# Attention with image prompts on one Trainium2 core: inner products sent through DRAM, and four smaller moves

## The chip, the core and the metric

The kernel runs on one of the eight cores of a Trainium2 chip. A core has four engines that compute, each with its own in-order instruction stream: TensorE (in the profile PE for products and PEld for loading their stationary operand), VectorE (DVE), ScalarE (ACT) and GpSimd (POOL). SyncE (SP) issues transfers. Transfers run on 16 DMA engines of the core; they are issued from the streams of SP, ACT or POOL. The metric is the device time of one execution in microseconds, the median of several runs. The profile shows one execution, taken by the hardware profiler.

## The reference

For each of 8 batch entries b there are 112 rows of x with 320 channels (20 heads of 16) and 375 rows of context with 512 features, the last four of which are image prompts. Everything is float32.

```
text, ip = ehs[:, :-4], ehs[:, -4:]                 # 371 and 4 rows
q = heads(x @ W_q);  k, v = heads(text @ W_k), heads(text @ W_v)
probs = softmax(q k^T / 4)                           # 112 x 371 for each head
text_out = probs v
attn_scores = q heads(ip @ W_k_ip)^T / 4             # 112 x 4
qsem = l2norm(probs text)                            # 112 x 512 for each head
sem  = qsem l2norm(ip)^T                             # 112 x 4
probs_ip = softmax(attn_scores + 0.5 sem) * mask
out = (text_out + probs_ip heads(ip @ W_v_ip)) @ W_out + b_out + x
```

The kernel never forms `probs text`. The squared norm of that row is p G p^T, where G is the 371 x 371 matrix of inner products of the text rows, and its product with the four normalised prompts needs only the inner products of text and prompts. So one product of p with a wide matrix [G, text times prompts, a column of ones, the head's values] gives the norm, `sem`, the sum of the exponentials and `text_out` together.

## The kernel before

The work is cut into 40 steps (b, g): 8 batch entries times 5 groups of 4 heads. The four heads of a group stand in the four quadrants of 32 partitions, so that their products run side by side.

For each b, `gram(b)` forms the upper triangle of G together with the prompts' columns on TensorE; `doubled` takes it out of PSUM with a factor of 2, and POOL multiplies the diagonal blocks by `half`. The result is `ug`, 128 partitions by 792 floats (`GW`; 3,168 bytes in a partition). The products want each 32-row block of `ug` in all four quadrants, so `gram_to_groups(b, blocks)` (L551) copies it into `u`: four transfers for each of the four blocks, 32 rows of 3,168 bytes each, from SBUF to SBUF. `values` makes the values, which go to DRAM (`vd`) and back by `values_to_groups` (L712) into `vr`, already split by quadrant; `placed` (L759, POOL) copies one group's 16 value columns behind the blocks in `u`.

For each step, `scores` (TensorE) and `probabilities` (DVE maximum, ACT exponential) give p. L821 on SP's queue places p's rows in a ring of two buffers, `xg`, one transfer a head, 28 partitions for each head. `transposed` (L823, DVE) turns `xg` by 32 x 32 blocks into `xgT`, in one piece, halves or other pieces of the 12 blocks. `multiplied` and `product` (L843) then run the 12 blocks of each head against `u`. `reduced` (DVE, L907) and `value_sums` (ACT, L881) take the sums out; `finish` ends a batch entry.

All streams are ordered by hand. The steps run in pairs: `pair(n)` works on steps n and n+1, issues the scores for n+2 and n+3, and calls `moved(b, g)` after the products of each step; `behind(n)` places the larger pieces (`k`, `v`, `gr`, `q`: keys, values, inner products, queries of coming entries) behind an even step. `moved` (L1373) issues the transfers for the next entry: for an even b block 0 after group 1, block 1 after group 2 and block 3 with the values after group 3; block 2 stands at the start of `behind`. For an odd b blocks 0 and 1 stand after groups 0 and 1, block 2 at the start of `behind` of group 1 and block 3 at its end after group 3. For entry 0 the blocks are sent in the prologue.

The prologue (L1206 to L1253) is ordered by hand too. `awake(n)` (L485) issues n products of a constant tile `waker` that nobody reads. `normalised_prompts` (L275) forms the norms of the 32 prompt rows (8 x 4) and turns the prompts twice, raw into `ipT` and normalised times 0.5 into `ipnT`; `prompt_projections` (L308) multiplies `ipT` by W_k_ip and W_v_ip much later, in `behind(0)`. The prologue calls `values_to_groups(0)` (L1235) on SP before the first group's scores and probabilities, whose rows go out on the same queue.

The waits that the prediction speaks of are at L854 (TensorE for `xgT` or `u`), at L763 (POOL for `u` or `vr`) and at L833 (DVE for `xg`).

Of the kernel before, what the change touches and what calls it, by code (L numbers as in the profile page):

```python
# [20 lines left out]
def kernel(  # L21
# [187 lines left out]

    halves(0)  # L210

    waker = const.tile([P, P], F32, tag="waker", name="waker")
    nc.vector.memset(waker, 1.0)

    hmask = const.tile([P, HC], F32, tag="hmask", name="hmask")
    nc.vector.tensor_reduce(
# [32 lines left out]
        for at in attn_ring:  # L249
            nc.gpsimd.memset(at[:, C:], 0.0)  # L250

    ipT = const.tile([P, NE, N], F32, tag="ipT", name="ipT")
    ipnT = const.tile([P, NE, N], F32, tag="ipnT", name="ipnT")
    kip = const.tile([P, NC, N], F32, tag="kip", name="kip")

# [19 lines left out]
    def normalised_prompts():  # L275

        sq = early[:, 1]
        ss = small.tile([N, 1], F32, tag="ipss", name="ipss", bufs=1)
        nc.vector.tensor_tensor_reduce(
            out=sq, in0=ip_sb, in1=ip_sb, scale=1.0, scalar=0.0, op0=ALU.mult, op1=ALU.add,  # L280
            accum_out=ss,
        )
        nc.vector.tensor_scalar_max(ss, ss, EPS * EPS)
        rn = small.tile([N, 1], F32, tag="iprn", name="iprn", bufs=1)
        yield

        ipn = early[:, 1]

        def turned_prompts(src, dst, n):
            ps = bank(f"ps_ipT{n}", spare=True)  # L290
            for e in range(NE):
                nc.tensor.transpose(
                    ps[:, e * N : (e + 1) * N], chunk(src, e), ident[:N, :N]
                )
            nc.vector.tensor_copy(
                dst, ps[:, : NE * N].rearrange("p (e n) -> p e n", n=N)
            )

        nc.scalar.activation(rn, ss, AF.Sqrt)
        turned_prompts(ip_sb, ipT, "r")  # L300
        nc.vector.reciprocal(rn, rn)
        nc.vector.tensor_scalar(ipn, ip_sb, rn, 0.5, op0=ALU.mult, op1=ALU.mult)
        yield

        turned_prompts(ipn, ipnT, "n")
        yield

    def prompt_projections():  # L308

        ps = bank("ps_kv")  # L310
        for e in range(NE):
            for i, w in enumerate((wkip_sb, wvip_sb)):
                for n, part in enumerate(parts):
                    m = 2 * i + n
                    nc.tensor.matmul(
                        ps[m * N : (m + 1) * N, : C // 2],
                        ipT[:, e, :],
                        w[:, e, part],
                        start=(e == 0),
                        stop=(e == NE - 1),  # L320
                    )
        kv = work.tile([P, CP], F32, tag="vip", name="kv", bufs=1)
        nc.scalar.copy(kv[:N, parts[0]], ps[:N, : C // 2])
        nc.scalar.copy(kv[:N, parts[1]], ps[N : 2 * N, : C // 2])
        nc.scalar.copy(kv[2 * N :, : C // 2], ps[2 * N :, : C // 2])
        nc.gpsimd.tensor_copy(kv[:N, C:], kv[:N, FULL * P : C])
        yield

        ps = bank("ps_kipT")
        for i in range(NC):  # L330
            nc.tensor.transpose(
                ps[:, i * N : (i + 1) * N], kv[:N, i * P : (i + 1) * P], ident[:N, :N]
            )
        nc.scalar.copy(kip, ps[:, : NC * N].rearrange("p (i n) -> p i n", n=N))
        for i in range(NC):
            nc.gpsimd.tensor_tensor(
                kipb[:, i],
                kip[:, i, :NIP].unsqueeze(1).to_broadcast([P, HC, NIP]),
                hmask.unsqueeze(2).to_broadcast([P, HC, NIP]),
                ALU.mult,  # L340
            )
        yield

        for n, part in enumerate(parts):
            m = 2 + n
            nc.sync.dma_start(vipd[:, part], kv[m * N : (m + 1) * N, : C // 2])
        yield
# [182 lines left out]
    def gram(b):  # L530
# [3 lines left out]
        for c in range(NT):  # L534
# [13 lines left out]
            doubled(ps, c, c, DEAL[c] if left_out(b, c) else ())  # L548
            yield

    def gram_to_groups(b, blocks, eng=nc.sync):  # L551

        for q in blocks:
            for a in range(GROUP):
                eng.dma_start(
                    st[b]["u"][a * RG : (a + 1) * RG, q * GW : (q + 1) * GW],
                    ug[q * RG : (q + 1) * RG, :],
                )
# [264 lines left out]
    def transposed(b, g, j0=0, j1=BLK):  # L823

        xg = x_ring[(b * NG + g) % NX]
        if j1 < j0 + 1:
            return
        if ("xT", g) not in st[b]:
            st[b]["xT", g] = work.tile([P, BLK, P], F32, tag="xgT", name=f"xgT_{b}_{g}")
        xT = st[b]["xT", g]  # L830
        n = BLK // (2 if b == B - 1 or (b, g) == (0, 0) or j1 - j0 < BLK else 1)
        for j in range(j0, j1, n):
            nc.vector.transpose(  # L833
                xT[:, j : j + n].rearrange("p j (k q) -> p q j k", q=QN),
                xg[:, :, j * RG : (j + n) * RG].rearrange("p q (j k) -> p q j k", k=RG),
            )
# [371 lines left out]
    products = first_gram()  # L1208
    next(prompts)
    nc.scalar.preload_act_table(AF.Sqrt)  # L1210
    awake(5)
    next(context)
    next(prompts)
    nc.scalar.preload_act_table(AF.Exp)
    load_query_weights(nc.gpsimd, range(1))
    next(context)
# [15 lines left out]
    run(("q", 0), lambda: project_queries(pairs[0]))  # L1232
    run(("k", 0), lambda: keys(0))
    run(("q", 0), None)
    values_to_groups(0)  # L1235
    for a in range(GROUP):
        scores(0, 0, a, early=True)
        probabilities(0, 0, a)
    run(("q", 0), None)
    run(("k", 0), None)  # L1240
    for a in range(GROUP):
# [63 lines left out]
    inputs = {5: (0, 2), 9: (2, 5), 19: (5, B)}  # L1305

    late = (1, 5)

    def pair(n):

        one, two = steps[n], steps[n + 1]
        b, g = one
        tags = ("mm", "sc") if b % 2 and g == NG - 1 else ("sc", "mm")
        ends = (BLK - 2, BLK - 1)

        products_in(b, g, ("qd",) * GROUP)
        for j in range(BLK - 2):
            product(b, g, j, range(GROUP))
            if j < 2:
                heads = (HIGH, LOW)[j]  # L1320
                coming_scores(n + LEAD, heads, tags[j])
                coming_probabilities(n + LEAD, heads)
            if j == 1:
                if n in late:
                    transposed(*two, 0, BLK // 2)
                transposed(*two, BLK // 2, BLK)
            if j % QN == QN - 1:
                placed(*two, (j // QN,))
        if n == 3:
            load_channels(nc.gpsimd, wo_sb, w_out)  # L1330
            nc.gpsimd.dma_start(sm_sb, smask.unsqueeze(1))
            nc.gpsimd.dma_start(bias_sb, b_out.partition_broadcast(S))
        if n in inputs:
            load_inputs(*inputs[n])
        products_in(*two, (tags[1],) * 2 + (tags[0],) * 2)
        for there, here in ((HIGH, LOW), (LOW, HIGH)):
            product(*two, 0, there)
            for j in ends:
                product(b, g, j, here)
        del st[b]["xT", g]  # L1340
        placed(*two, (NT - 1,))
        moved(b, g)
        if g > 1 and g != 2:
            turned(b + 2)
        if b % 2 and g in (0, NG - 1):
            f(b - 1 - (g == 0))
        if g in (1, 2):
            f(b - 1, 2)
        reduced(b, g)
        if g == 2:  # L1350
            turned(b + 2)
        value_sums(b, g)
        if b % 2 == 0 and b > 0 and g == 1:
            turned_inputs(pairs[b // 2 + 1], 0, FULL)

        b, g = two
        for j in range(1, BLK - 2):
            product(b, g, j, range(GROUP))
            if j == 4:
                coming_scores(n + 1 + LEAD, HIGH, "qd")  # L1360
                coming_probabilities(n + 1 + LEAD, HIGH)
            if j == 7:
                coming_scores(n + 1 + LEAD, LOW, "qd")
                coming_probabilities(n + 1 + LEAD, LOW)
        for heads in (HIGH, LOW):
            for j in ends:
                product(b, g, j, heads)
        del st[b]["xT", g]
        moved(b, g)
        if one in ((b, 2), (b, 3)):  # L1370
            turned(b + 2, 1 + (one == (0, 3)))

    def moved(b, g):  # L1373

        nb = b + 1
        if b % 2 == 0:
            if g in (1, 2):
                gram_to_groups(nb, (g - 1,))
            if g == 3:
                todo = [lambda: gram_to_groups(nb, (3,)), lambda: values_to_groups(nb)]  # L1380
                for move in reversed(todo) if nb == B - 1 else todo:
                    move()
        else:
            if g in (0, 1):
                gram_to_groups(nb, (g,))
            if g == 2:
                values_to_groups(nb, 0, 2)

    def behind(n):
# [4 lines left out]

        def tr(i):
            if i < len(two):
                transposed(*two[i], 0, BLK // (1 + i))

        if b % 2 == 0 and g == 0:
            if n == 0:  # L1400
# [257 lines left out]
```

## Time and profile before

| | us |
|---|---|
| median of 3 runs | 405.58 |
| lowest and highest run | 403.81 and 406.58 |
| profiled execution, its own time | 403.29 |
| its span, first to last instruction | 401.6 |
| ACT busy | 200.2 |
| POOL busy | 192.5 |
| `u<-ug` on SP's queue | 120 transfers |

The profiled execution was a little faster than the runs shown. Rows of a timeline begin with the start and the duration in microseconds, then the engine, the line, the operation, what is written from what, and the shapes; brackets tell the idle time before and what ended it. The letter q behind an engine's name (SPq) means that the row is the issue of a transfer, not its work. A row of the transfers gives how many were issued and the size of each. A row of the windows gives for a stretch its length, the busy time of each engine, TensorE's granted clock, the share of the 16 DMA engines that was busy and the rate in GB/s.

### The profile page before, as it was taken

To read this page: it belongs to the slowest core of one execution; us is meant where nothing else is said; L and a number is where in the kernel's file an instruction comes from. 1 tells how busy PE (TensorE), PEld (TensorE's weight loads), DVE (VectorE), ACT (ScalarE), POOL (GpSimd) and SP (SyncE) were. 2 spreads that over 40 slices of the span, in tenths; PEclk is the share of its full clock that TensorE was granted. 3 is DMA by queue.
4 is the path that set the end of the run, shared out by engine and by line. 5 is a ranking of instruction groups with operands and counts; after the bars stand their busy time and mean duration, and the time that the engine had idled before them with its cause. 6 is when DMAs were issued, how large, how long until landed. Compare 5 with 4: busy or idle time off the path is not lost.

```text
span 401.6 us, 14442 instructions
## 1 busy us (share of the span) xinstructions
PE 396.1 (99%) x5685; PEld 320.2 (80%) x5685; DVE 332.2 (83%) x712; ACT 200.2 (50%) x716; POOL 192.5 (48%) x409
## 2 busy tenths in 40 slices
PE   8999999999999999999999999999999999999996
PEld 8768697888878788878787878877887878887894
DVE  4357689877989988987999898897798988888995
ACT  3255343347434853425652665334843485446864
POOL 8655427052562567051573348432256155804781
PEclk9999999999999999999999999999999999999999
DMA  8979657988577846668657766576846544775321
GB/s 239 217 202 258 155 153 178 210 193 190 149 186 155 202 122 187 155 146 184 169 148 167 193 155 169 160 185 140 191 120 175 130 125 116 197 176 166 108 59 29
DMA packets 58119, 65.86 MB, mean 164 GB/s; under 512 B 20165, under 2 KB 51257, under 8 KB 58052
## 3 DMA queue, kind: packets, MB, share of 16 engines
q1 hardware_dynamic: 54814, 58.23, 57.7%
q0 software_dynamic: 2544, 5.92, 6.0%
q8 instruction: 45, 0.74, 0.9%
q10 hardware_dynamic: 694, 0.80, 0.6%
q14 instruction: 22, 0.18, 0.2%
HBM read 20.22 MB, written 5.22 MB: 63 GB/s over the span
## 4 chain that ended last, share of the span: by engine, by line
PE 96%; DVE 2%; ACT 1%; issue 0%; DVEq 0%
PE ps_qd L854 47%; PE ps_k L571 10%; PE ps_g L541 8%; PE ps_s L797 6%; PE ps_v L613 6%; PE ps_vs L671 6%; PE ps_k L588 3%; PE ps_q L402 3%; PE ps_o L1050 2%; PE ps_g L503 1%; DVE xgT L833 1%; PE ps_w L489 1%; PE ps_c L472 1%; PE ps_q L384 1%; PE ps_a L1041 0%
## 5 line engine op out<-in xcount | busy, mean ns | idle before, releaser
L854 PE MATMUL ps_qd<-u,xgT 32*112 32x72 f32 (+10 forms) x3806 | 216.0, 352 | 0.8 <-DVE xgT L833 0.7
L854 PEld LDWEIGHTS ps_qd<-u,xgT 32*112 32x112 f32 x3806 | 177.5, 172 | 33.5 <-issue 4.2
L833 DVE STREAM_TRANSPOSE xgT<-xg 128x768 f32<-128x768 f32 (+1 forms) x63 | 123.1, 1973 | 4.3 <-DMA xg<-p 4.1
L814 ACT ACTIVATE p<-ps_s,nmx 112x371 f32<-112x371 f32 x160 | 85.5, 585 | 64.9 <-DVE nmx L810 63.9
L810 DVE TENSOR_REDUCE nmx<-ps_s 112x1 f32<-112x371 f32 x160 | 76.8, 534 | 26.2 <-PE ps_s L797 24.6
L763 POOL COPY u<-vr 128x64 f32<-128x64 f32 x120 | 26.9, 237 | 140.8 <-PE ps_qd L854 76.8
L907 DVE CUSTOM_DVE_ANT_0 p<-ps_qd,p 112x371 f32<-112x371 f32 x148 | 71.6, 540 | 10.0 <-ACT pvs L881 7.4
L797 PE MATMUL ps_s<-kT,qm 32*112 32x375 f32 (+1 forms) x320 | 61.0, 485 | 0.0
L881 ACT COPY pvs<-ps_qd 112x21 f32<-112x21 f32 x148 | 21.3, 200 | 52.5 <-DVE ss L907 49.9
L571 PE MATMUL ps_k<-ctxT,wk_sb 128*128 128x371 f32 x128 | 43.4, 482 | 0.0
L571 PEld LDWEIGHTS ps_k<-ctxT,wk_sb 128*128 128x128 f32 x128 | 23.1, 190 | 12.8 <-issue 0.8
L541 PE MATMUL ps_g<-ctxT 128*32 128x119 f32 (+11 forms) x672 | 32.7, 338 | 0.0
L541 PEld LDWEIGHTS ps_g<-ctxT 128*32 128x32 f32 x672 | 27.7, 109 | 6.1 <-issue 1.2
L797 PEld LDWEIGHTS ps_s<-kT,qm 32*112 32x112 f32 x320 | 27.3, 171 | 6.3 <-POOL vext L675 1.1
L460 DVE STREAM_TRANSPOSE ctxT<-ct 128x512 f32<-128x512 f32 x21 | 22.5, 1081 | 6.7 <-DMA ct<-in_ctx_dram 6.7
L816 ACT COPY ipl<-ps_s 112x4 f32<-112x4 f32 x140 | 24.3, 174 | 0.0
L613 PE MATMUL ps_v<-wv_sb,ctxT 128*128 128x320 f32 x80 | 23.6, 442 | 0.0
L613 PEld LDWEIGHTS ps_v<-wv_sb,ctxT 128*128 128x128 f32 x80 | 14.5, 190 | 5.6
L578 ACT COPY kT<-ps_k 128x371 f32<-128x371 f32 x16 | 7.5, 469 | 22.2 <-PE ps_k L571 22.2
L1029 POOL TENSOR_TENSOR vip<-vip,w 112x1280 f32<-112x1280 f32 (+1 forms) x8 | 17.5, 2182 | 0.2 <-DVE w L1023 0.2
L525 POOL TENSOR_TENSOR ug<-ug,half 128x128 f32<-128x128 f32 (+1 forms) x24 | 10.7, 451 | 14.3 <-ACT ug L524 13.0
L520 ACT ACTIVATE ug<-ps_g 128x279 f32<-128x279 f32 (+5 forms) x24 | 8.0, 333 | 17.5 <-PE ps_g L541 10.8
(189 smaller groups left out, 469.1 us busy)
## 6 DMA issues: line engine op xcount, KB each, us to landing
xg<-p SPq DMA_DIRECT2D x159, 162.3 KB
u<-ug SPq DMA_DIRECT2D x120, 99.0 KB
ct<-in_ctx_dram SPq DMA_DIRECT2D x28, 176.0 KB
vip<-vipd SPq DMA_DIRECT2D x7, 560.0 KB
vr<-vd SPq DMA_DIRECT2D x20, 120.0 KB
out_dram<-ob SPq DMA_DIRECT2D x7, 140.0 KB
vd<-vext POOLq DMA_DIRECT2D x12, 80.0 KB, 3.4
vr<-vd SPq DMA_DIRECT2D x12, 80.0 KB
```

Of the source, the lines that this page charges most:

```text
L541: nc.tensor.matmul(ps[p * RG : (p + 1) * RG, s0 : T - t0], ctxT[:, e, t0 + q * RG : t0 + (q + 1) * RG], ctxT[:, e, t0 + s0 : T], start=(e ...
L571: nc.tensor.matmul(ps[:, :TT], wk_sb[:, e, i * P : (i + 1) * P], s["ctxT"][:, e, :TT], start=(e == 0), stop=(e == NE - 1),)
L613: nc.tensor.matmul(ps[:, :C], ctxT[:, e, c * P : (c + 1) * P], wv_sb[:, e, :], start=(e == 0), stop=(e == NE - 1),)
L671: nc.tensor.matmul(ps[:, :CH], a[:, k], t[:, k], start=(k == 0), stop=(k == 1))
L763: nc.gpsimd.tensor_copy(region(b, c)[:, :, UV - c * P :], s["vr"][:, c * QN : (c + 1) * QN, g, :])
L797: nc.tensor.matmul(ps[:S, :w], qm[a * RG : (a + 1) * RG, i, r, j * S : (j + 1) * S], s["kT"][a * RG : (a + 1) * RG, i, :w], start=True, st ...
L810: nc.vector.tensor_reduce(nmx, ps[:S, :TT], AX.X, ALU.max, negate=True)
L814: nc.scalar.activation(p, ps[:S, :TT], AF.Exp, bias=nmx)
L816: nc.scalar.copy(s["ipl"][:, groups[g][a], :], ps[:S, TT:T])
L833: nc.vector.transpose(xT[:, j : j + n].rearrange("p j (k q) -> p q j k", q=QN), xg[:, :, j * RG : (j + n) * RG].rearrange("p q (j k) -> p ...
L854: nc.tensor.matmul(banks[a][:S, j * RG : UW], xT[a * RG : (a + 1) * RG, j, :S], region(b, c)[a * RG : (a + 1) * RG, p, q * RG :], start=(j ...
L907: nc.vector.tensor_tensor_reduce(out=p, in0=ps[:S, :TT], in1=p, scale=1.0, scalar=0.0, op0=ALU.mult, op1=ALU.add, accum_out=s["ss"][:, h : ...
```

## The change

Five things are changed.

- Inner products by way of DRAM, for b > 0: a new `gram_to_dram(b)` writes the whole of `ug` to a DRAM tile `ud` in one transfer, where block 0 used to be sent (after group 1 for an even b, group 0 for an odd b). `gram_to_groups` then reads each block with one transfer that repeats the block's 32 rows four times. Blocks 0 and 1 are issued together, one step of a pair later; block 2 follows at the start of `behind` and block 3 stays.
- The first group's scores, probabilities and row transfers come before `values_to_groups(0)`.
- `transposed` for step 3 is cut: a quarter (3 of 12 blocks) is turned in `pair(1)` behind `reduced`, the other 9 blocks in one piece in `behind(2)`.
- The waking products read a constant that the framework has in SBUF instead of a tile written by DVE. There are 7 in place of 5, and 1 more later.
- The raw prompts are not turned. The projections use the normalised prompts and are scaled by twice the norm as they leave PSUM.

```diff
-    waker = const.tile([P, P], F32, tag="waker", name="waker")
-    nc.vector.memset(waker, 1.0)
+    waker = nc.const_aps.tensor(1.0, [P, P], F32)
...
-        nc.scalar.activation(rn, ss, AF.Sqrt)
-        turned_prompts(ip_sb, ipT, "r")
-        nc.vector.reciprocal(rn, rn)
+        nc.scalar.activation(norms[:N], ss, AF.Sqrt)
+        nc.vector.reciprocal(rn, norms[:N])
         nc.vector.tensor_scalar(ipn, ip_sb, rn, 0.5, op0=ALU.mult, op1=ALU.mult)
...
+        nc.vector.tensor_scalar_mul(norms[:N], norms[:N], 2.0)
+        for k in range(1, P // N):
+            nc.vector.tensor_copy(norms[k * N : (k + 1) * N], norms[:N])
...
-                        ipT[:, e, :],
+                        ipnT[:, e, :],
...
-        nc.scalar.copy(kv[:N, parts[0]], ps[:N, : C // 2])
-        nc.scalar.copy(kv[:N, parts[1]], ps[N : 2 * N, : C // 2])
-        nc.scalar.copy(kv[2 * N :, : C // 2], ps[2 * N :, : C // 2])
+        for to, own in (
+            (kv[:N, parts[0]], slice(0, N)),
+            (kv[:N, parts[1]], slice(N, 2 * N)),
+            (kv[2 * N :, : C // 2], slice(2 * N, P)),
+        ):
+            nc.scalar.mul(to, ps[own, : C // 2], norms[own])
...
+    def gram_to_dram(b):
+
+        st[b]["ud"] = dram.tile([P, GW], F32, tag="ud", name=f"ud_{b}")
+        nc.sync.dma_start(st[b]["ud"], ug)
+
     def gram_to_groups(b, blocks, eng=nc.sync):
 
         for q in blocks:
+            if b > 0:
+                eng.dma_start(
+                    st[b]["u"][:, q * GW : (q + 1) * GW],
+                    st[b]["ud"][q * RG : (q + 1) * RG].unsqueeze(0).to_broadcast([GROUP, RG, GW]),
+                )
+                continue
...
         n = BLK // (2 if b == B - 1 or (b, g) == (0, 0) or j1 - j0 < BLK else 1)
+        if (j1 - j0) % n:
+            n = j1 - j0
...
-    awake(5)
+    awake(7)
     next(context)
     next(prompts)
+    awake(1)
...
-    values_to_groups(0)
     for a in range(GROUP):
         scores(0, 0, a, early=True)
         probabilities(0, 0, a)
+    values_to_groups(0)
...
         reduced(b, g)
+        if n in ahead:
+            transposed(*steps[n + 2], 0, BLK // 4)
...
-            if g in (1, 2):
-                gram_to_groups(nb, (g - 1,))
+            if g == 1:
+                gram_to_dram(nb)
+            if g == 2:
+                gram_to_groups(nb, (0, 1))
...
-            if g in (0, 1):
-                gram_to_groups(nb, (g,))
+            if g == 0:
+                gram_to_dram(nb)
+            if g == 1:
+                gram_to_groups(nb, (0, 1))
...
-                transposed(*two[i], 0, BLK // (1 + i))
+                done = BLK // 4 if n - 1 in ahead and i == 0 else 0
+                transposed(*two[i], done, BLK // (1 + i))
```

`ahead` is `(1,)`.

More of the change, by code (lines that the diff above doesn't have):

```diff
@@ L250, in more_constants @@
             nc.gpsimd.memset(at[:, C:], 0.0)
-    ipT = const.tile([P, NE, N], F32, tag="ipT", name="ipT")
+    norms = const.tile([P, 1], F32, tag="norms", name="norms")
     ipnT = const.tile([P, NE, N], F32, tag="ipnT", name="ipnT")
@@ L285, in normalised_prompts @@
         yield
+        nc.scalar.activation(norms[:N], ss, AF.Sqrt)
+        nc.vector.reciprocal(rn, norms[:N])
         ipn = early[:, 1]
[L289 to L297, printed above, removed]
-        nc.scalar.activation(rn, ss, AF.Sqrt)
-        turned_prompts(ip_sb, ipT, "r")
-        nc.vector.reciprocal(rn, rn)
         nc.vector.tensor_scalar(ipn, ip_sb, rn, 0.5, op0=ALU.mult, op1=ALU.mult)
         yield
-        turned_prompts(ipn, ipnT, "n")
+        ps = bank("ps_ipT", spare=True)
+        for e in range(NE):
+            nc.tensor.transpose(ps[:, e * N : (e + 1) * N], chunk(ipn, e), ident[:N, :N])
+        nc.vector.tensor_copy(ipnT, ps[:, : NE * N].rearrange("p (e n) -> p e n", n=N))
         yield
     def prompt_projections():
+        nc.vector.tensor_scalar_mul(norms[:N], norms[:N], 2.0)
+        for k in range(1, P // N):
+            nc.vector.tensor_copy(norms[k * N : (k + 1) * N], norms[:N])
         ps = bank("ps_kv")
@@ L1307 @@
     late = (1, 5)
+    ahead = (1,)
     def pair(n):
```

## The prediction

> **What bounds the kernel now.** I read the page first: span, busy time by engine, and the chain of work that ended last.
>
> ```profile
> span 401.6 us, 14442 instructions
> PE 396.1 (99%) x5685; PEld 320.2 (80%) x5685; DVE 332.2 (83%) x712; ACT 200.2 (50%) x716; POOL 192.5 (48%) x409
> ...
> PE 96%; DVE 2%; ACT 1%; issue 0%; DVEq 0%
> ```
>
> TensorE is busy all the time and is 96% of the chain. A saving elsewhere is worth nothing unless TensorE stands still for it, so the next view is what TensorE waits for.
>
> ```profile
> PE ps_qd L854 <- DVE xgT L833: 0.7, 1, 0.7
> ```
>
> (Engine, tile and line waited for: us in total, times, longest.) Beside the start, this is the only wait of its size inside the work, so removed waits can give about 1 us at most, beside TensorE's own instructions. What can be lost is not bounded like that: any transfer that comes later than TensorE needs it is paid in full. The change must be read from that side.
>
> **The change, part by part.**
>
> *Start.*
>
> ```profile
> 0.91 0.17 DVE L213 MEMSET waker<- 128x128 f32 x1 [0.91 <-PEq L1640]
> 1.13 2.50 PE L489 MATMUL ps_w<-waker 128*128 128x128 f32 x10 [1.13 <-DVE waker L213]
> 3.60 1.10 PE L472 MATMUL ps_c<-ident,ct 128*128 128x128 f32 x4
> 4.63 0.66 PE L292 MATMUL ps_ipTr<-ident,wvt 32*128 32x32 f32 x4
> 5.22 0.74 PE L472 MATMUL ps_c<-ident,ct 128*128 128x128 f32 x4
> 47.20 1.89 DVE L810 TENSOR_REDUCE nmx<-ps_s 112x1 f32<-112x371 f32 x4 [3.79 <-PE ps_s L797]
> ```
>
> Without the memset TensorE can begin up to 0.2 us earlier (1.13 - 0.91). Seven waking products in place of five are 4 more instructions at 0.25 (2.50 / 10), 1.0 us, and `awake(1)` is 2 more, 0.25 to 0.5 us. Against that go the four turnings of the raw prompts, 0.66, and the first four turnings (1.10) may take what the second four take (0.74) if they come later after the waking: 0.36. Sum: +1.0 + 0.4 - 0.2 - 0.66 - 0.36 = +0.2, or +0.4 with the products on the dear side. The other bound is -0.6: all that is added hides behind the wait for the context, and the 0.66 goes. I take the middle, -0.1. The copy of `ipT` (DVE), the one scaled copy in place of a plain one (ACT, three times) and four small DVE instructions on `norms` lie off TensorE: the copies of the projections come just before 47.20, where DVE has been idle for 3.79, so they cost 0; were that cover gone, four small ones at 0.1 to 0.2 would be some 0.6 us.
>
> The Trainium skill ("TensorE: Matmul & The Clock Gate", section The HAM clock gate) says that the array runs at half clock until about 3.4 us of sustained activity, in a free-running window. The rows agree with it (the same four turnings take 1.10, then 0.74); by it an earlier first product brings the fast clock earlier by at most the same 0.2 us, or not at all, which lies within the bounds above.
>
> *First placements ahead of the values' loads.*
>
> ```profile
> 23.79 1.87 SPq L716 DMA_DIRECT2D vr<-vd  x4
> 25.76 5.50 SPq L821 DMA_DIRECT2D xg<-p  x6
> 28.00 0.24 POOL L763 COPY u<-vr 128x64 f32<-128x64 f32 x1 [3.27 <-DMA vr<-vd]
> 32.37 3.08 DVE L833 STREAM_TRANSPOSE xgT<-xg 128x768 f32<-128x768 f32 x2 [2.47 <-DMA xg<-p]
> 34.19 1.22 PE L854 MATMUL ps_qd<-u,xgT 32*112 32x392 f32 x10
> ```
>
> The four issues of `vr` (1.87) stand on SP's queue ahead of the rows of group 0; without them the rows leave up to 0.8 earlier (they still wait for the exponentials), the turning at 32.37 starts as much earlier, and its first half (1.54) no longer ends just before the product at 34.19: gain 0.1 to 0.2. `vr` in turn is issued 4 x 0.92 later than the rows begin, near 28.6, and by its own time from issue to use (28.00 - 23.79 = 4.2) is there at 32.8: placed 33.1, 1.1 us before it is needed. POOL's in-order work behind that placement (loading of x, memsets, the halving of the inner products) moves by the same 5 us; its next consumer is `gram_to_dram`, near 52, so 0.
>
> *A quarter of the turning moved.*
>
> ```profile
> 54.76 0.99 DVE L810 TENSOR_REDUCE nmx<-ps_s 112x1 f32<-112x371 f32 x2 [1.01 <-PE ps_s L797]
> 59.48 3.01 DVE L833 STREAM_TRANSPOSE xgT<-xg 128x1536 f32<-128x1536 f32 x1
> 60.65 1.30 PE L402 MATMUL ps_q<-xT,wq_sb 128*128 128x224 f32 x6
> 62.64 1.22 PE L854 MATMUL ps_qd<-u,xgT 32*112 32x392 f32 x10 [0.69 <-DVE xgT L833]
> ```
>
> This is the 0.7 us. TensorE is free at 61.95 and waits for the turning of (0,3). A quarter of it (3.01 / 4 = 0.75) now runs in DVE's hole of 1.01 before 54.76. If the rows of (0,3) are there when the hole opens, all 0.69 go; if they come at its end, the maxima behind it and the chain to 59.48 are pushed by up to 0.75 and nothing is won. I take the middle, 0.3.
>
> *Inner products by way of DRAM, seven times.* SP's issues go from 16 to 5 for each b; SP's time is not on the path: 0. The question is when they land.
>
> ```profile
> xg<-p SPq DMA_DIRECT2D x159, 162.3 KB
> u<-ug SPq DMA_DIRECT2D x120, 99.0 KB
> ...
> vr<-vd SPq DMA_DIRECT2D x20, 120.0 KB
> 35.00:40.00 5.00, 5.00 (x102) 4.10 (x95) 4.50 (x6) 2.32 (x8) 0.82 (x5) 1.00 1.01 307
> 38.00:39.00 1.00, 1.00 (x36) 1.00 (x32) 1.00 (x1) 0.38 (x1) 0.05 (x1) 1.00 0.98 410
> 98.00:106.00 8.00, 8.00 (x89) 6.71 (x91) 7.83 (x12) 4.73 (x15) 5.45 (x11) 1.00 0.64 165
> 0.81 1.32 ACTq L160 DMA_DIRECT2D wvt<-in_ctx_dram  x1
> 3.88 0.68 DVE L279 CUSTOM_DVE_ANT_0 wvt<-wvt 32x512 f32<-32x512 f32 x1 [1.78 <-DMA wvt<-in_ctx_dram]
> ```
>
> (The window rows end with the share of the 16 DMA engines and GB/s.) A block is now one transfer of 4 x 99.0 KB whose source begins with a repeat of 4, then 32 rows. Before, a transfer had 32 rows outermost. The trace does not show how a source that begins with 4 is shared out among 16 engines, so two bounds: all 16 share it (as now), or each of 4 engines takes one repeat, 99 KB. The row nearest to it is the load of the prompts, whose source begins with 8: 64 KB, issued at 0.81 and there at 3.88, while the context's first chunk of 256 KB, issued at the same 0.81 with 128 rows outermost, lets TensorE begin at 3.60. A quarter of the bytes takes 3.1 against 2.8, so I take 4 engines; the row only leans that way.
>
> The Trainium skill ("DMA: Bandwidth & Descriptors", sections Rules for kernel authors and How many engines) says that a leading zero-stride broadcast of c copies confines a whole transfer to at most c engines, the lowest-numbered ones. The row just named agrees with its sense, but no row counts the engines.
>
> Price on 4 engines. One engine moves GB/s / (16 x share): 26.1 at best (38:39), 19.0 (35:40), 16.1 (98:106). I take their mean, 20.4. I assume that an engine serves what SP has issued in order, so that transfers issued behind the blocks wait for them on these four engines.
>
> ```profile
> 59.62 5.02 SPq L555 DMA_DIRECT2D u<-ug  x8
> 98.23 5.03 SPq L555 DMA_DIRECT2D u<-ug  x8
> 152.20 5.13 SPq L555 DMA_DIRECT2D u<-ug  x8
> 193.00 5.03 SPq L555 DMA_DIRECT2D u<-ug  x8
> 343.18 5.32 SPq L555 DMA_DIRECT2D u<-ug  x8
> 82.35 0.93 PE L854 MATMUL ps_qd<-u,xgT 32*112 32x392 f32 x8
> 119.43 1.22 PE L854 MATMUL ps_qd<-u,xgT 32*112 32x392 f32 x10
> 177.81 1.22 PE L854 MATMUL ps_qd<-u,xgT 32*112 32x392 f32 x10
> 214.44 1.22 PE L854 MATMUL ps_qd<-u,xgT 32*112 32x392 f32 x10
> 363.89 1.22 PE L854 MATMUL ps_qd<-u,xgT 32*112 32x392 f32 x10
> ```
>
> The first five rows are where three blocks will be issued together for b = 0, 1, 2, 3 and 6, the others the products that come next and need what lies in that queue.
> Even b: before the first product of b+1 one engine must move four blocks (396 KB), four `xg` (a 14th of 162.3 KB each, taking it that 28 rows are dealt to 14 engines: 46) and `vr` (4 x 120 / 16 = 30): 472 KB of 1,024 bytes, 23.7 us. With 0.8 for the issue and 0.24 for the placement: 84.4 against 82.35, +2.0; 176.9 against 177.81, 0 (b = 4 lies as b = 2 does); 367.9 against 363.89, +4.0.
> Odd b: three blocks (297), `vd` (30) and the four `xg` (46) that the turning (3.0) ahead of the product needs: 373 KB, 18.7 us. 117.7 against 119.43 - 3.0, +1.3; 212.5 against 211.4, +1.1; b = 5 has more room, 0.
> Sum +8.4. The same at 26.1 gives 0, at 22.5 (middle of the two faster windows) 1.8, at 19.0 17, at 16.1 47. The new write of `ug` to DRAM (396 KB on 16 engines) is issued half a pair earlier and costs 0 while it lands within that time; a late one would hold up SP, with the `xg` queued behind it.
>
> **Sum.** -0.1 - 0.2 - 0.3 + 8.4 = +7.8. The profiled execution took 403.29 us (span 401.6), which gives 411.1. The median of the runs shown, 405.58, is 2.3 longer; on it, 413.4, which I forecast.
>
> **The rivals.** (a) *Sixteen engines share a block after all.* Speaks for it: `u<-ug` does so now, and nothing in the trace counts engines. Then a block's 396 KB land no later than the four transfers do now, and -0.6 remains: 405.0, not slower. This is the other side; it decides by one thing, how many engines a block uses.
> (b) *Four engines, but hidden.* The blocks are large rows, read by engines that idle otherwise; at 22.5 GB/s the sum is 1.8 - 0.6, at 26.1 it is -0.6: 405 to 410 with what lies between, say 407. For it: four engines that work alone should come nearer the best window than the mean; against it: the places at 82.35 and 363.89 have the least room.
> (c) *`vr` late at the start.* If it lands after 34.0 in place of 32.8, TensorE waits at its first product; at 2 us late 405.6 + 0.8 = 406.4. Against it: 1.1 us of room.
>
> **How the numbers follow.** More than about 1%, 4 us, can be told from no change. Forecast 0.57 (413.4; its own range 409.6 to 432), (a) 0.13 (405.0), (b) 0.25 (407), (c) 0.05 (406.4). Slower by over 1%: 0.57. Same: 0.25 + 0.05 + 0.10 of (a); faster: 0.03 of (a). The range runs from (a) less the 1 us by which runs scatter, 404, to a third of the way from the value at 19.0 GB/s (405.6 + 17 - 0.6 = 422) to that at 16.1 (452), 432.
>
> **What would show it.** Right: POOL's placement (L763) waits for `u<-ud` or `vr` up to the first product of an odd b, with TensorE idle there 3 to 5 us, most near the last; TensorE waits for turned blocks after the bursts; issue to landing of a block 5 us and more. Wrong: TensorE's waits as short as now. The quarter is right if the 0.69 wait shrinks; the start if the first product comes before 34.19. The forecast is wrong above all if a block is spread over more than four engines, or if four of them move it at 22.5 GB/s or faster.

## The result, and the profile after

The changed kernel takes 483.76 us (median of 6 runs, 479.79 to 488.33) where the kernel before takes 406.37 (6 runs): a ratio of 1.1891, 95% interval 1.182 to 1.1962. The ratio leaves out the slowest run of each, which lies over 1.5% above its fastest. The profiled execution took 479.79 us, its span is 478.1. The forecast, 413.4 with a range of 404 to 432, had the sign and some of the places of the loss, but a tenth of its size.

The page of the changed kernel: span, busy time, TensorE's granted clock in 40 slices (tenths of full speed), and the chain that ended last by engine.

```profile
span 478.1 us, 14320 instructions
PE 413.4 (86%) x5687; PEld 336.3 (70%) x5687; DVE 331.2 (69%) x715; ACT 201.0 (42%) x716; POOL 191.9 (40%) x409
PEclk9999999699997999869998999979999799995999
PE 54%; DMA 33%; SPq 4%; DVE 3%; issue 2%; POOL 2%; ACT 2%; POOLq 0%; DVEq 0%
```

TensorE was 96% of the chain before; now it is 54%, and transfers are 33%. The 76.5 us of added span split into two parts. TensorE stands still for 64.7 us (478.1 - 413.4) where it stood for 5.5 (401.6 - 396.1): +59.2. And it is busy for 413.4 us in place of 396.1 with two more instructions: +17.3, its products have become slower. The clock row points to the reason: it has dents, each behind a wait.

From the table of waits, what TensorE and POOL waited for (us in total, times, longest):

```profile
POOL u L770 <- DMA vr<-vd: 66.4, 5, 18.8
PE ps_qd L863 <- POOL u L770: 34.5, 6, 11.1
POOL u L770 <- DMA u<-ud: 33.8, 2, 21.0
PE ps_g L537 <- POOL ctxT L444: 19.2, 2, 9.7
PE ps_qd L863 <- DVE xgT L842: 5.1, 3, 1.8
PE ps_kipT L327 <- ACT p L821: 1.2, 1, 1.2
```

The four TensorE rows sum to 60.0. The two of `ps_qd` are of the kinds that were forecast: POOL's placement (now L770) waits for `vr` or a block, TensorE for the placement, or for turned rows. The row of `ps_g`, in which TensorE waits for a copy into `ctxT`, was not forecast, and that of `ps_kipT` belongs to the quarter turning.

The timeline around the first block transfers, those of entry 1 (start, duration, engine, line, work; in brackets the idle time before and what ended it; SPq rows are issues):

```profile
61.98 1.78 SPq L556 DMA_DIRECT2D u<-ud  x3
77.88 0.57 SPq L556 DMA_DIRECT2D u<-ud  x1
82.23 3.97 SPq L723 DMA_DIRECT2D vr<-vd  x4
93.76 0.59 POOL L770 COPY u<-vr 128x64 f32<-128x64 f32 x3 [16.49 <-DMA vr<-vd]
94.05 2.25 PE L863 MATMUL ps_qd<-u,xgT 32*112 32x392 f32 x10 [10.30 <-POOL u L770]
```

From the first block's issue to the placement pass 31.8 us; the forecast allowed 24.8 (59.62 to 84.4). Block 3 leaves 16 us after the first three, and `vr` only at 82.23.

### The profile page after: what moved, and what is told of

The parts are those of the page before. It is cut to its first block, busy times and chain, and to the rows that moved or that the text cites. A ratio compares the mean times of both kernels' runs of the same rounds, so it can differ in the third digit from the quotient of the medians.

```text
span 478.1 us, 14320 instructions
## 1 busy us (share of the span) xinstructions
PE 413.4 (86%) x5687; PEld 336.3 (70%) x5687; DVE 331.2 (69%) x715; ACT 201.0 (42%) x716; POOL 191.9 (40%) x409
## 4 chain that ended last, share of the span: by engine, by line
PE 54%; DMA 33%; SPq 4%; DVE 3%; issue 2%; POOL 2%; ACT 2%; POOLq 0%; DVEq 0%
PE ps_qd L863 27%; DMA u<-ud 15%; DMA vr<-vd 8%; DMA xg<-p 6%; PE ps_g L537 6%; PE ps_k L578 5%; PE ps_v L620 4%; PE ps_s L804 3%; PE ps_vs L678 3%; DMA vd<-vext 3%; PE ps_k L595 2%; SPq L828 2%; DVE xgT L842 1%; SPq L723 1%; PE ps_g L499 1%
## 5 line engine op out<-in xcount | busy, mean ns | idle before, releaser
L863 PE MATMUL ps_qd<-u,xgT 32*112 32x72 f32 (+9 forms) x3806 | 228.5, 366 | 39.7 <-POOL u L770 34.5
L863 PEld LDWEIGHTS ps_qd<-u,xgT 32*112 32x112 f32 x3806 | 189.3, 179 | 73.0 <-POOL u L770 35.9
L842 DVE STREAM_TRANSPOSE xgT<-xg 128x768 f32<-128x768 f32 (+2 forms) x64 | 122.1, 1927 | 50.1 <-DMA xg<-p 50.0
L770 POOL COPY u<-vr 128x64 f32<-128x64 f32 x120 | 26.9, 239 | 221.9 <-PE ps_qd L863 84.7
L916 DVE CUSTOM_DVE_ANT_0 p<-ps_qd,p 112x371 f32<-112x371 f32 x148 | 71.6, 539 | 16.5 <-PE ps_qd L863 8.7
L804 PE MATMUL ps_s<-kT,qm 32*112 32x375 f32 (+1 forms) x320 | 63.4, 502 | 0.0
L537 PE MATMUL ps_g<-ctxT 128*32 128x119 f32 (+11 forms) x672 | 36.7, 365 | 19.2 <-POOL ctxT L444 19.2
L537 PEld LDWEIGHTS ps_g<-ctxT 128*32 128x32 f32 x672 | 30.3, 115 | 26.8 <-POOL ctxT L444 20.2
L804 PEld LDWEIGHTS ps_s<-kT,qm 32*112 32x112 f32 x320 | 28.9, 179 | 6.1 <-POOL vext L682 1.4
```

The costliest lines, as they stand in the source:

```text
L537: nc.tensor.matmul(ps[p * RG : (p + 1) * RG, s0 : T - t0], ctxT[:, e, t0 + q * RG : t0 + (q + 1) * RG], ctxT[:, e, t0 + s0 : T], start=(e ...
L770: nc.gpsimd.tensor_copy(region(b, c)[:, :, UV - c * P :], s["vr"][:, c * QN : (c + 1) * QN, g, :])
L804: nc.tensor.matmul(ps[:S, :w], qm[a * RG : (a + 1) * RG, i, r, j * S : (j + 1) * S], s["kT"][a * RG : (a + 1) * RG, i, :w], start=True, st ...
L842: nc.vector.transpose(xT[:, j : j + n].rearrange("p j (k q) -> p q j k", q=QN), xg[:, :, j * RG : (j + n) * RG].rearrange("p q (j k) -> p ...
L863: nc.tensor.matmul(banks[a][:S, j * RG : UW], xT[a * RG : (a + 1) * RG, j, :S], region(b, c)[a * RG : (a + 1) * RG, p, q * RG :], start=(j ...
L916: nc.vector.tensor_tensor_reduce(out=p, in0=ps[:S, :TT], in1=p, scale=1.0, scalar=0.0, op0=ALU.mult, op1=ALU.add, accum_out=s["ss"][:, h : ...
```

## The experiments

Each kernel ran beside the kernel before on the same chip; ratios are to it, with 95% intervals. The theory after the result: a block on four engines takes so long that everything behind it is late. Rivals: the way through DRAM itself, the order on SP's queue, one of the four smaller moves.

**One repeat, two, four.** In `four_reads` a block is read by four transfers of 32 rows, in `two_repeats` by two transfers that repeat it twice. The diff shows both; each kernel has one of the two loops.

```diff
-                eng.dma_start(
-                    st[b]["u"][:, q * GW : (q + 1) * GW],
-                    st[b]["ud"][q * RG : (q + 1) * RG].unsqueeze(0).to_broadcast([GROUP, RG, GW]),
-                )
+                for a in range(GROUP):                      # four_reads
+                    eng.dma_start(
+                        st[b]["u"][a * RG : (a + 1) * RG, q * GW : (q + 1) * GW],
+                        st[b]["ud"][q * RG : (q + 1) * RG],
+                    )
+                for a in range(0, GROUP, 2):                # two_repeats
+                    eng.dma_start(
+                        st[b]["u"][a * RG : (a + 2) * RG, q * GW : (q + 1) * GW],
+                        st[b]["ud"][q * RG : (q + 1) * RG].unsqueeze(0).to_broadcast([2, RG, GW]),
+                    )
```

> The changed kernel, but each block is read from ud by four transfers of 32 rows each, in place of one that repeats the 32 rows four times. The way through DRAM, its order and its places in the queue stay. Theory (few engines: the repeat confines a block to four engines): the blocks share 16 engines, three of them land within 6 us in place of 15 to 20, the waits for u and vr go, 403 to 409 us. Rival (the way through DRAM, the write and the later joint issue, is what costs): 470 to 490 us. Rival (the order on SP's queue, with transfers behind the blocks held up): between, 430 to 470 us, since SP now issues 16 transfers per entry in place of 4.

> The changed kernel, but each block is read by two transfers that repeat its 32 rows twice. Theory (the leading count of repeats sets the number of engines, and they are the same ones for each transfer): two engines at about 20 GB/s each, so three blocks (1188 KB) take about 29 us in place of 15, each entry loses 10 to 20 us more, 550 to 620 us. Rival (a repeat of any count is slow as such, or the two transfers use different engines): the rate in a burst stays near 80 GB/s and the time at 475 to 490 us.

`four_reads`: 405.51 us, ratio 1.001 (0.9971 to 1.0048). The whole loss is gone, with the way through DRAM, the late joint issue and more issues on SP's queue still there. `two_repeats`: 592.05 us in one run; the loss grows with the same bytes and half as many repeats in a transfer. The windows show the engines themselves. A row has its stretch, its length, five engines' busy time, TensorE's granted clock, the share of the 16 DMA engines that was busy, and GB/s. First the changed kernel, while the blocks of entry 1 are under way:

```profile
78.00:80.00 2.00, 2.00 (x19) 1.10 (x21) 1.55 (x6) 0.47 (x1) 0.00 (x0) 1.00 0.26 100
80.00:82.00 2.00, 2.00 (x37) 1.70 (x30) 0.00 (x0) 0.06 (x1) 0.00 (x0) 1.00 0.26 100
```

then `two_repeats`, a little later, with the blocks of entry 1 still under way:

```profile
90.00:95.00 5.00, 0.00 (x0) 0.00 (x0) 0.00 (x0) 0.00 (x0) 0.00 (x0) 0.50 0.14 47
```

and `four_reads`, with its first blocks on their way:

```profile
63.00:68.00 5.00, 5.00 (x69) 3.78 (x71) 4.93 (x9) 1.50 (x6) 4.10 (x9) 1.00 0.90 251
```

Behind the same three issues and at the same place, first the changed kernel and then `four_reads`:

```profile
64.00:66.00 2.00, 2.00 (x29) 1.22 (x32) 1.96 (x3) 0.00 (x0) 2.00 (x5) 1.00 0.26 90
64.00:66.00 2.00, 2.00 (x28) 1.22 (x32) 2.00 (x3) 0.00 (x0) 2.00 (x5) 1.00 0.88 231
```

0.26 of 16 is 4.2 engines, 0.14 is 2.2, 0.90 is 14.4. One engine moves 100 / 4.2 = 24 GB/s in the first and 47 / 2.2 = 21 in the second. So, at both counts that were run, the number of repeats in front of the source is the number of engines that are busy, and two such transfers do not use different engines. The Trainium skill ("DMA: Bandwidth & Descriptors", section Rules for kernel authors) states that a leading repeat of c copies confines a transfer to at most c engines; the trace agrees with it at two counts.

**The parts apart.** `dram_alone` is the kernel before with the way through DRAM alone, `four_moves` the changed kernel without it. The diff shows one place of each; the other entries and `gram_to_groups` go with it.

```diff
-            if g in (1, 2):                # dram_alone, against before
-                gram_to_groups(nb, (g - 1,))
+            if g == 1:
+                gram_to_dram(nb)
+            if g == 2:
+                gram_to_groups(nb, (0, 1))
...
-            if g == 1:                     # four_moves, against after
-                gram_to_dram(nb)
-            if g == 2:
-                gram_to_groups(nb, (0, 1))
+            if g in (1, 2):
+                gram_to_groups(nb, (g - 1,))
```

> The kernel before with the way through DRAM alone, as in the changed kernel. Theory (all of the loss is there): 480 to 487 us. Rival (the parts add up otherwise, for instance because the quarter turning delays the first burst): 460 to 478 us.

> The changed kernel without the way through DRAM: blocks go from SBUF to SBUF, in the order and places of before; the other four parts stay. Theory: the four parts together are worth -0.6 us, 404.5 to 406.5 us. Rival (one of them, the first placements or the quarter turning, costs part of the loss): above 410 us.

`dram_alone`: 481.99 us, 1.1914 (1.1813 to 1.2015), all of the loss. `four_moves`: 407.76 us, 1.0053 (1.0021 to 1.0086), so the other four parts together cost 0.8 to 3.5 us where the theory said a gain of 0.6. Its table of waits shows the one new wait of its size on TensorE:

```profile
PE ps_kipT L327 <- ACT p L810: 1.3, 1, 1.3
```

In this execution that wait is followed by a stretch of half clock:

```profile
58.05 0.37 PE L327 MATMUL ps_kipT<-ident,kv 32*128 32x32 f32 x3 [1.27 <-ACT p L810]
59.40:62.80 3.40, 3.40 (x15) 3.40 (x14) 3.32 (x9) 1.49 (x9) 1.26 (x6) 0.50 0.63 173
```

So the wait of 1.27 us costs about 1.7 us more (3.40 x 0.50). The changed kernel waits 1.16 at the same place and stays at 1.00 behind it.

**The quarter turning, taken out and alone.** `no_quarter` is `four_moves` with `ahead = ()`, `quarter_alone` is the kernel before with the quarter.

```diff
-    ahead = (1,)
+    ahead = ()
```

> The four moves without the quarter turning: start, first placements and prompts as in the changed kernel, blocks from SBUF to SBUF. Theory (the quarter waits for rows that come late and holds the maxima, the exponentials and ScalarE's copy behind it; it cost 2.4 us of TensorE's time near 58): 404.5 to 406 us, no difference from before, and the wait of 0.7 us near 62 is back. Rival (the loss of the four moves lies in the first placements or the start): 407 to 409 us, as the four moves.

> The kernel before with the quarter turning alone. Theory (the quarter stands ahead of the maxima in VectorE's order and waits for the rows of step 3): TensorE waits about 1 us near 58 and the time rises by 1 to 2.5 us, 406.5 to 408 us. Rival (the quarter is harmful only together with the later placements, which delay those rows by 1 us): no difference or up to 0.7 us gained, 404.5 to 405.5 us.

405.48 us, 1.0017 (0.9984 to 1.0049), and 406.23 us, 1.0022 (0.9988 to 1.0057). Neither can be told from no change, and their intervals overlap that of `four_moves`; the times don't settle what the quarter costs. The traces show the mechanism. In the changed kernel:

```profile
56.48 0.86 DVE L842 STREAM_TRANSPOSE xgT<-xg 128x384 f32<-128x384 f32 x1 [2.19 <-DMA xg<-p]
57.20 1.82 DVE L817 TENSOR_REDUCE nmx<-ps_s 112x1 f32<-112x371 f32 x4
57.72 1.96 ACT L821 ACTIVATE p<-ps_s,nmx 112x371 f32<-112x371 f32 x4 [3.21 <-DVE nmx L817]
58.34 0.37 PE L327 MATMUL ps_kipT<-ident,kv 32*128 32x32 f32 x3 [1.16 <-ACT p L821]
```

The quarter waits for rows that land late, at 56.48; the maxima stand behind it on DVE and start at 57.20 (54.76 before); the exponentials wait for them, and with them ScalarE's queue, on which the scaled projections `kv` stand that TensorE turns at L327. So the 0.69 near 62 went and 1.2 came. In `quarter_alone` the rows of TensorE show no such wait, against what its theory expected: the wait takes the quarter together with another of the moves. That is the rival's condition; that it is the later placements is not shown.

**The start alone.** `start_alone` is `no_quarter` with the first placements as before. `reads_start` has that start too, and reads blocks as `four_reads` does.

```diff
+    values_to_groups(0)
     for a in range(GROUP):
         scores(0, 0, a, early=True)
         probabilities(0, 0, a)
-    values_to_groups(0)
```

> The kernel before with the new start alone (waking products from the constant, raw prompts not turned, projections scaled). Theory: -0.1 us (bounds -0.6 to +0.4), no measurable difference, 404 to 406 us. Rival (the larger number of waking products delays the first context): above 406.5 us.

> The changed kernel without the quarter turning and with the first placements as before, and each block read from ud by four transfers of 32 rows. Theory (on 16 engines the way through DRAM is neither better nor worse, since TensorE waits for no block in either kernel): 404 to 406 us, no difference from before. Rival (the blocks issued together and from DRAM give the other transfers more room): 401 to 403.5 us.

406.26 us, 1.0022 (0.9988 to 1.0056), and 404.81 us, 0.9989 (0.9958 to 1.0021): no difference in either. No version here beats the kernel before, and its page says why: there were 5.5 us in all in which TensorE was idle.

**Why the loss is 59 us of waiting and not 8.** Two kernels change what stands behind a late transfer. In `copy_elsewhere` the copy of the prompts into `ctxT` runs on DVE; in `block3_early` block 3 leaves with blocks 0 and 1.

```diff
-        nc.gpsimd.tensor_copy(                             # copy_elsewhere
+        (nc.vector if b > 0 else nc.gpsimd).tensor_copy(
             st[b]["ctxT"][:, :, TT:T], ipnT[:, :, b * NIP : (b + 1) * NIP]
         )
...
-                gram_to_groups(nb, (0, 1))                 # block3_early
+                gram_to_groups(nb, (0, 1, 3))
...
-            gram_to_groups(nb, (3,))
```

> The changed kernel with the copy of the normalised prompts into ctxT on VectorE in place of POOL, for b > 0. Theory (the room was short because that copy stands on POOL behind the placement that waits for vr, and the inner products of the next entry need it): for b = 3 and 5 TensorE no longer stops ahead of the inner products but 7 us of work later, at the first product, and the waits of 9.7 and 9.5 us there fall by 5 to 8 us each: 468 to 476 us. Rival (the transfers alone set the time, whatever is behind them): 480 to 488 us.

> The changed kernel with block 3 issued together with blocks 0 and 1 in place of after group 3. Theory (part of the loss is that block 3 starts late and then needs 5 to 8 us on its four engines): the second wait of even b (4.1, 3.2 and 5.4 us) goes, the waits ahead of odd b shrink by 2 to 5 us each, 450 to 468 us. Rival (only the bytes on four engines count): 478 to 488 us.

`copy_elsewhere`: 470.7 us, 1.1613 (1.1557 to 1.1669), which lies below the changed kernel's interval. What it removed is seen at entry 3, first in the changed kernel:

```profile
204.20 0.59 POOL L770 COPY u<-vr 128x64 f32<-128x64 f32 x3 [18.82 <-DMA vr<-vd]
204.73 0.20 POOL L444 COPY ctxT<-ipnT 128x16 f32<-128x16 f32 x1
204.99 1.62 PE L537 MATMUL ps_g<-ctxT 128*32 128x375 f32 x9 [9.67 <-POOL ctxT L444]
```

and in `copy_elsewhere`:

```profile
197.38 4.65 PE L537 MATMUL ps_g<-ctxT 128*32 128x375 f32 x96
206.36 0.59 POOL L770 COPY u<-vr 128x64 f32<-128x64 f32 x3 [18.85 <-DMA vr<-vd]
206.65 1.73 PE L863 MATMUL ps_qd<-u,xgT 32*112 32x392 f32 x8 [4.61 <-POOL u L770]
```

`vr` is as late as ever, but the inner products of the next entry no longer stand behind the placement, and TensorE's wait falls from 9.67 to 4.61 (at entry 5 from 9.54 to 5.09). `block3_early`: 480.13 us, 1.1839 (1.1784 to 1.1893), no different from the changed kernel. The theory expected 450 to 468 and fell. The waits ahead of odd entries are at most 1.1 us shorter. The second waits of the even entries went, but the first ones grew: over the three entries they are 22.6 us, where both together were 17.7 in the changed kernel. The row of the table, and the wait at entry 2, 7.82 in place of 1.80 and 4.07:

```profile
PE ps_qd L863 <- DVE xgT L842: 22.6, 3, 9.0
140.63 2.25 PE L863 MATMUL ps_qd<-u,xgT 32*112 32x392 f32 x10 [7.82 <-DVE xgT L842]
```

With block 3 sent earlier, TensorE waits for the turned rows instead. That fits the rival, that the bytes on the four engines count and not their order; no run separates it from the waits on SP's queue.

**Slower products.** `kept_awake` puts 40 idle products ahead of the first product of an odd entry. They stood only ahead of entry 1; entry 7 is not run by `pair`, so half of the expectation was not tried.

```diff
+        if n in (5, 35):
+            awake(40)
```

> The changed kernel with 40 idle products of the constant tile ahead of the first product of b = 1 and b = 7, where TensorE waits for 10 to 11 us. Theory (besides standing still, TensorE runs the first 4 to 5 us after such a wait at a granted clock of 0.50 to 0.53, about 2 us lost each time): the granted clock right behind these two waits is 1.0 and the first products take 1.2 us per 10 in place of 2.25, some 4 us gained in all, 478 to 482 us. Rival (the slower products come from something else, such as the transfers that run at that time): the products there stay slow, 483 to 486 us.

484.3 us, 1.1919 (1.1844 to 1.1994): one place of 2 us is below what the runs tell, and in this execution the placement itself came 2.0 us later (96.04 against 94.05). The windows tell it. The changed kernel behind its wait of 10.30, then `kept_awake` at the same work:

```profile
94.00:98.00 4.00, 3.95 (x28) 2.74 (x32) 0.99 (x2) 0.43 (x1) 3.92 (x9) 0.53 0.93 158
98.00:102.00 4.00, 4.00 (x94) 3.81 (x89) 3.86 (x5) 1.86 (x8) 1.77 (x6) 1.00 0.36 105
```

```profile
94.00:98.00 4.00, 2.20 (x27) 1.75 (x29) 0.37 (x1) 0.00 (x0) 2.17 (x6) 1.00 0.99 194
96.04 1.22 PE L863 MATMUL ps_qd<-u,xgT 32*112 32x392 f32 x10 [1.80 <-POOL u L770]
```

After the wait the clock is 0.53 for some 4 us and the first ten products take 2.25; with the wait filled it is 1.00 and they take 1.22, though the transfers are as busy there (0.99 against 0.93). So a long wait is paid a second time, by about 4.0 x (1 - 0.53) = 1.9 us.

## Why the prediction was right in its sign and wrong in its size

**Engines.** Right. The step "I take 4 engines; the row only leans that way" rested on a weak row, as it said; 0.26 and 0.14 show it. So is the price: 20.4 GB/s for one engine lies just below the 21 and 24 of windows in which blocks run.

**What is late next.** Right for odd entries 1 and 7, where TensorE stops at the first product behind the placement: 10.30 and 11.11 us for +2.0 and +4.0. The sum failed in four steps.

(1) *"an engine serves what SP has issued in order", from one issue of everything to the end, at 20.4 GB/s.* 472 KB took 31.0 us from issue to placement for entry 1 (61.98 + 0.8 to 93.76) and 29.2 for entry 3 (174.18 + 0.8 to 204.20), 15.6 and 16.5 GB/s, not 20.4; that is about the slowest of the prediction's three rates, 16.1. The transfers were not all in the queue. SP itself stood, which the forecast had put at "SP's time is not on the path: 0". SP's own waits in the changed kernel:

```profile
SPq L828 <- DMA u<-ud: 18.9, 9, 4.8
SPq L723 <- DMA u<-ud: 15.1, 5, 4.0
SPq L556 <- DMA u<-ud: 5.4, 1, 5.4
```

By these rows SP held back rows, `vr` and block 3 for 39.4 us in all until an earlier block had landed; before there is one such row, of 0.2. In `four_reads`, with more issues in the same order, the same rows sum to 0.4, so SP stood because the blocks were slow. What ties those issues to the blocks is not shown. Other traffic on the same four engines adds to it. How the 5.5 to 7.3 us over the forecast's 23.7 divide between the two was not separated; `block3_early`, with all four blocks issued together, won nothing.

(2) *The deadline.* The prediction measured the room up to the first product of the next odd entry. For b = 3 and 5 the room ends earlier, as the rows of the kernel before show, which it did not read:

```profile
172.35 0.59 POOL L763 COPY u<-vr 128x64 f32<-128x64 f32 x3 [9.01 <-DMA vr<-vd]
172.89 0.20 POOL L448 COPY ctxT<-ipnT 128x16 f32<-128x16 f32 x1
173.22 3.12 PE L541 MATMUL ps_g<-ctxT 128*32 128x375 f32 x44
```

Before the change `vr` already came just in time: POOL had waited 9 us for it, and TensorE used the copy behind the placement 0.13 us after its end (at entry 5 1.25 us after, with the inner products at 268.69 and the first product at 273.28). The deadline was 173.22, not 177.81. That is 4.6 us for each of two entries; with them the forecast of 176.9 would have been a wait of about 4, and the 5 us of step 1 make the 9.67. `copy_elsewhere` shows this part: with the copy gone, TensorE runs on up to the first product.

(3) *Block 3 of the even entries.* For odd b the sum held three blocks; the fourth leaves last, when TensorE is 4 us from the products that need it (135.64 to 143.69 - 4.07). The changed kernel at entry 2:

```profile
134.53 1.22 PE L863 MATMUL ps_qd<-u,xgT 32*112 32x392 f32 x10 [1.80 <-DVE xgT L842]
135.64 0.63 SPq L556 DMA_DIRECT2D u<-ud  x1
143.40 0.41 POOL L770 COPY u<-vr 128x64 f32<-128x64 f32 x2 [12.81 <-DMA u<-ud]
143.69 1.85 PE L863 MATMUL ps_qd<-u,xgT 32*112 32x392 f32 x14 [4.07 <-POOL u L770]
```

The forecast +1.3 is the first wait, 1.80; the second, 4.07 (3.24 and 5.37 at entries 4 and 6), was not in the sum.

(4) *The clock.* No term stood for it, though the prediction quoted the rule for the start. TensorE's busy time rose by 17.3 us over seven waits of 3.24 us and more. The windows from the end of each wait to the end of the half clock behind it, the longest one and the sum over all seven:

```profile
258.73:265.02 6.29, 6.29 (x56) 5.36 (x60) 2.73 (x9) 0.71 (x4) 1.42 (x5) 0.50 0.82 186
sum 33.77, PE 33.77 PEld 26.07 DVE 10.83 ACT 3.47 POOL 13.85; mean PE 4.82 PEld 3.72 DVE 1.55 ACT 0.50 POOL 1.98
```

The clock is 0.50 in each of the seven, so about half of 33.77 is lost, 16.9 us or 2.4 a wait: nearly all of the 17.3. (Kernels without such waits differ by some 3 us in busy time, 396.1 before and 399.0 in `four_reads`.) `kept_awake` shows the cause at one place, with 1.9 us. The Trainium skill ("TensorE: Matmul & The Clock Gate", section HAM oscillation) says that idle gaps above about 3.4 us let the clock fall, each time anew. The trace agrees for the gap of 10.30; it shows the same behind the one of 3.24 us (the row of 258.73), a little under that figure, 5 us after another of 1.45. Shorter ones did it too: 1.27 in `four_moves`, above, and 2.74 in `kept_awake`, where the first ten products took 2.25 again:

```profile
367.71 2.25 PE L863 MATMUL ps_qd<-u,xgT 32*112 32x392 f32 x10 [2.74 <-DVE xgT L842]
```

In the changed kernel a wait of 1.80 did not. What decides between them is not shown.

Together: the waits ahead of odd entries sum to 10.30 + 9.67 + 9.54 + 11.11 = 40.6 (forecast 6.0), those of even entries to 5.1 + 12.7 = 17.7 (forecast 2.4), the clock to 17.3 (forecast 0). The term that was mis-sized most is the rate in step 1: the prediction itself said that its sum is 47 at 16.1 GB/s, about the rate that was measured from issue to placement. With that rate and the two earlier deadlines of step 2 (2 x 4.6) its sum is an estimated 56, against 58.4 us of waits measured. The clock is most of the rest.

**The small parts.** *Start*: taken as -0.1 within -0.6 and +0.4. TensorE begins at 0.85 in place of 1.13, but the sign that was named, a first product before 34.19, did not come (34.74), and `start_alone` is no different. *Quarter*: taken as -0.3, with the bad case "pushed by up to 0.75". The 0.69 went, but the maxima were pushed by 2.4, because the rows themselves came later (SP issued them at 49.56, before at 48.37); +0.5 on TensorE. *First placements*: taken as -0.2, placement at 33.1. In the changed kernel:

```profile
31.35 3.14 DVE L842 STREAM_TRANSPOSE xgT<-xg 128x768 f32<-128x768 f32 x2 [1.37 <-DMA xg<-p]
34.45 0.59 POOL L770 COPY u<-vr 128x64 f32<-128x64 f32 x3 [9.60 <-DMA xg<-p]
34.74 1.22 PE L863 MATMUL ps_qd<-u,xgT 32*112 32x392 f32 x10 [0.40 <-POOL u L770]
```

The turning starts 1.0 us earlier, as forecast; the placement comes 1.35 later than forecast and TensorE waits for it 0.40 us. That is the wait of rival (c); but the row names the rows `xg`, not `vr`, as what POOL waited for last, so that a late `vr` caused it is not shown. A saving ahead of one input of a product only shows the other.

**The rivals.** (a), sixteen engines, is refuted by the shares; what it says of time is what `four_reads` gives. (b), hidden, is refuted: its condition, 22.5 GB/s or faster, did come true in a window (24), and the blocks were not hidden, so the rate in a window was the wrong thing to make it hang on.

## What to carry to other kernels

Look at the order of dimensions of a transfer before its size or count: here one transfer with a repeat of 4 in front got 4 of 16 engines, and four transfers of the same bytes with 32 rows in front got nearly all. When a transfer becomes slower, the deadline is not the first instruction that reads it but the first that stands behind its reader in any in-order queue; follow the reader's engine down its rows. Add to each longer wait of TensorE the slower products behind it: here 2.4 us on average for each of seven waits of 3.24 us and more, and in single cases for shorter ones too.

## What the runs showed of the hardware

A repeat of 4 in front of the source kept 0.26 of the DMA engines busy at 100 GB/s, a repeat of 2 kept 0.14 busy at 47 GB/s. A wait of 3.24 us was followed by a granted clock of 0.50 over the next 6.29 us, one of 1.27 us (in another kernel) by 0.50 over 3.4 us, and one of 1.80 us by none; 9.2 us of idle products in a wait, with 1.80 left of it, kept the clock at 1.00.
